# Graph layer on one core: row sums stored by SyncE instead of added by GpSimd, and a fifth of the lookup tables kept in SBUF

## The chip, the cores and the metric

One core of a Trainium2 chip runs the whole program. The metric is the device time of one execution in microseconds; the kernel before has a median of 24819.2 us over 10 runs (24803.0 to 24842.31). Engines are named as in the profile: PE is TensorE (matmul), PEld its weight loads, DVE VectorE, ACT ScalarE, POOL GpSimd, SP SyncE. SP computes nothing; it issues DMAs, as ACT and POOL can. "L391" is line 391 of the kernel before.

## The reference

A graph with 100000 nodes of 64 features has 3.3 million edges (1.6 million random pairs in both directions and one loop per node), sorted by the node they point to (`dst`). Each node's features are normalised and clipped at zero (`h`); the mean over a node's incoming edges goes through a linear layer, and is added to the input:

```python
h = jnp.maximum(_layernorm(x, axis=-1), 0.0)
local, nbr = h[dst], h[src]
y = jnp.einsum('ec,oc->eo', jnp.concatenate([local, nbr - local], axis=-1), W) + b
s = segment_sum(y, dst, 100000)
cnt = segment_sum(ones, dst, 100000)[:, None]
x = x + jnp.where(cnt > 0, s / jnp.maximum(cnt, 1.0), 0.0)
```

Since the layer is linear, what has to be summed over edges is only `h[src]` and a count: for each node the sum of some 33 rows picked at random from a table of 100000 rows.

## The kernel before, in words

**Stage 1, rows** (L269 to L310). `h` is computed and written to HBM as `h3`: each row is the float32 value split in three bf16 parts of 64, and ones for the count, 194 values (`CT`) of which 193 (`CE`) are used. A float32 array `acc` of 65 columns (64 sums and a count) is filled with zeros. At the end of the program `acc` is turned into means, multiplied by the weights and added to `x` (L983 to L1019).

The edges are summed in two ways at the same time.

**Chunks** (`chunks`, L345). The last 1.26 million edges are cut in 352 chunks of 3584 (28 columns of 128). For each column POOL issues an indirect DMA that gathers 128 rows of `h3` into `nb` (L391); DVE makes a one-hot matrix `hot` of the targets relative to the chunk's first node; PE multiplies the two into PSUM (`ps`, L396). A chunk covers at most 128 neighbouring nodes. Its base, the first node, is in `base_r` and `base_b`. When a chunk is done DVE reduces `ps` to `sums` (L407, L409), and later `addition` adds these 128 rows to `acc` by a POOL DMA with accumulation: an indirect one in the prologue (L366), one with a start row read from `base_r` in the loop (L371). The index arrays of a group of `KG` = 16 chunks are loaded at once (`load`, L348), two chunks ahead of their use. `nb` has 6 buffers of half a chunk (14 columns).

**Windows** (`quads`, L740). The first 2.04 million edges are cut in 256 windows of 7968 edges; a window covers at most 256 nodes (`CH`). Four windows make a set, of which there are 64. The edges of a window were sorted by their source in two lanes (`sort_lane`, mostly DVE and ACT) and spread out into index arrays in HBM (`fill_lane`; it also uses POOL gathers). For a set the kernel walks over all of `h3` in 157 steps of 640 rows, two steps at a time: the rows come as a table `tab` by SP (three steps in one load, 53 loads per set, L761); DVE makes one-hot matrices `gh` (L789) and `dh` (L340) from `srs` and `dt`, which SP loads too; PE picks the wanted rows (`gp`, L811, 12 matmuls for two steps), ACT copies them to `gs` (L813), and PE adds them to the four windows' sums (`total`, L819, 32 matmuls for two steps). At the end of a set DVE makes the four `wsums` (L839 to L845), and `addition` (L847) adds 256 rows of each to `acc` by a POOL DMA with accumulation (L849), from the start row in `wb_r`. `load` buffers are three deep, and SP's loads are issued 8 steps ahead (`AHEAD`).

**The order.** All engines run their instructions in the order in which the program emits them; only semaphores order the engines against one another. `chunks` is a generator that yields after each gather; the other stages call it to interleave gathers with their own work. In the prologue `gathers(ns)` (L873) emits one gather for each `GATHER` = 1250 ns of estimated work; a double step of the first four sets counts 2 x `STEP`. The prologue is: the two lanes' sort with chunks beside it (lane 1 also fills lane 0), then the sets 0 to 3 (`U0`) with the filling of lane 1, then `drain(ev)` emits what is left of the prologue's chunks (`PA`, 58 of them), and `add_now(True)` the additions. Then a loop runs three times (L909), each with 20 sets (`SB`) and 98 chunks (`KB`), the chunks' gathers spread evenly over the sets' steps, and at its end `drain` and `add_now(True)`; between two turns all engines meet.

Additions are put off: `add_later(due, ...)` queues one until 56 more gathers are emitted ((`LAG` - 1) x `J`), and `add_now` emits at most one in `GAP` = 8 gathers. `number` (L318) reads a start row into a register of the engine named. `odd` collects flags for inputs that don't fit the plan (a window with too many nodes and the like); if one is set, a loop at the end clears `acc` and does all edges again in a simple way (L937 and L947, zero turns here).

Of the kernel before, what the change touches and what calls it, by code (L numbers as in the profile page):

```python
# [27 lines left out]
P = 128  # L28
P = 128
# [5 lines left out]
KB = 98  # L35
U0 = 4
KG = 16
# [3 lines left out]
STEP = 1050  # L41
GAP = 8
# [52 lines left out]
def gnn_preln(ctx: ExitStack, tc, x, src_w, dst_w, src_p, dst_p, src_a, dst_a, wT, b, out, V, E):  # L95
# [50 lines left out]
    wb_d = dram.tile([SETS * W, 1], I32, name="wb_d")  # L146
# [28 lines left out]
    wb_r = consts.tile([1, SETS * W], I32, name="wb_r")  # L175
    turns = consts.tile([1, 2], I32, name="turns")
    ones = consts.tile([P, 1], F32, name="ones")
# [4 lines left out]
    odd = consts.tile([P, 1 + 5 * LANES], F32, name="odd")  # L182
# [129 lines left out]
    with tc.tile_pool(name="rows", bufs=6) as rows, \  # L312
# [5 lines left out]
        def number(at, engine, most):  # L318
            with tc.issue_after(last[engine].ins):
                return nc.values_load(at, engines=[engine], min_val=0, max_val=most)  # L320
# [5 lines left out]
        later = []  # L326
        count = [0, 0]
# [17 lines left out]
        def chunks(first, n, dynamic=None):  # L345


            def load(q):  # L348
# [11 lines left out]
                to = index.tile([P, KG], I32, name="to", bufs=3)  # L360
                nc.vector.tensor_scalar(to[:, :k], base_b[:, at], pcol, None, op0=ALU.add)
                return si, near, to

            def addition(q, rows_to, sums):
                if dynamic is None:
                    nc.gpsimd.indirect_dma_start(  # L366
                        out=acc, out_offset=bass.IndirectOffsetOnAxis(ap=rows_to, axis=0),
                        in_=sums, in_offset=None, compute_op=ALU.add)
                else:
                    at = number(base_r[0:1, ds(dynamic + q, 1)], POOL, V)  # L370
                    nc.gpsimd.dma_start(acc[ds(at, P)], sums, accum_op=ALU.add)  # L371
# [4 lines left out]
            for k in range(n * parts + 1):  # L376
                q, part = divmod(k, parts)
                u = q % KG
                if q < n:
                    if u == 0 and part == 0:  # L380
                        si, near, to = ahead
                    hot = rows.tile([P, JH, P], BF16, name="hot", bufs=4)
                    nb = rows.tile([P, JH, CT], BF16, name="nb")
                    with behind():
                        one_hot(hot, near[:, u, part * JH:part * JH + JH], P)
# [18 lines left out]
                if before is not None and before[2] == parts - 1:  # L404
                    sums = rows.tile([P, C1], F32, name="sums", bufs=LAG + 2)
# [4 lines left out]
                    add_later((LAG - 1) * J, lambda b=before[3], s=sums: addition(*b, s))  # L410
                if q < n:
                    before = (hot, nb, part, (q, to[:, u:u + 1]))
# [5 lines left out]
        def sort_lane(l, keys, piece, few, ps):  # L418
# [5 lines left out]
            nc.vector.tensor_scalar_min(wb[:, 0:1], wb[:, 0:1], float(V - CH))  # L424
# [315 lines left out]
        def quads(base, n):  # L740
# [4 lines left out]
            def fetch(t):  # L745
# [12 lines left out]
                if s < NCB and s % TG == 0:  # L758
# [4 lines left out]
                if s == NE // 2:  # L763
                    owns[u] = load.tile([P, W, NT, CT], BF16, name="own", bufs=1)
                    for i in range(W):
                        at = number(wb_r[0:1, ds((base + u) * W + i, 1)], SP, V - CH)
# [56 lines left out]
            def put(t):  # L823
# [12 lines left out]
                for i in range(W):  # L836
# [10 lines left out]
                    def addition(w=(base + u) * W + i, sums=sums):  # L847
                        at = number(wb_r[0:1, ds(w, 1)], POOL, V - CH)
                        nc.gpsimd.dma_start(acc[ds(at, CH)].rearrange("(b p) c -> p b c", p=P), sums, accum_op=ALU.add)  # L849

                    add_later((LAG - 1) * J, addition)
# [17 lines left out]
        with tc.tile_pool(name="few", bufs=1) as few:  # L869
# [14 lines left out]
            with tc.tile_pool(name="keys", bufs=2) as big, tc.tile_pool(name="piece", bufs=2) as piece, \  # L884
                    tc.tile_pool(name="fill", bufs=2) as fill, tc.tile_pool(name="sort_ps", bufs=2, space=PSUM) as ps:
                for l in range(NL):
                    rest = fill_lane(l - 1, fill, took) if l else iter(())
                    for i, ns in enumerate(sort_lane(l, big.tile([P, WL], F32, name="keys"), piece, few, ps)):
# [5 lines left out]
                        gathers(ns)  # L894
# [3 lines left out]
            with tc.tile_pool(name="load", bufs=3) as load, tc.tile_pool(name="hots", bufs=3) as hots, \  # L898
# [9 lines left out]
                add_now(True)  # L908
                with tc.For_i(0, (SETS - U0) // SB, 1) as g:  # L909
                    ev = chunks(None, KB, PA + g * KB)  # L910
                    next(ev)
                    owed = 0.0
                    for _ in quads(U0 + g * SB, SB):
# [5 lines left out]
                    add_now(True)  # L919

    with tc.tile_pool(name="few", bufs=1) as few, tc.tile_pool(name="w_ps", bufs=1, space=PSUM) as wps:
        worst = few.tile([P, 1], F32, name="worst")
# [136 lines left out]
```

## Time and profile before

The profile shows one execution. It took 24811.12 us, and the span of its instructions, from the first to the last, is 24809.4 us; the median of the 10 runs is 24819.2 us. Cut by what runs:

| stretch, us from the start | us | what runs | PE matmuls | POOL busy, us | granted PE clock | DMA, GB/s |
|---|---|---|---|---|---|---|
| 0 to 437 | 437 | rows | 1569 | 205 | 0.75 | 290 |
| 437 to 2720 | 2283 | sort, lanes 0 and 1, beside it 1267 gathers | 1190 | 1517 | 0.52 | 63 |
| 2720 to 4084 | 1364 | sets 0 to 3, beside it 284 gathers | 14408 | 526 | 0.74 | 176 |
| 4084 to 4201 | 117 | drain, 73 gathers | 162 | 83 | 0.54 | 35 |
| 4201 to 10968 | 6767 | loop, turn 1 | 73424 | 2868 | 0.75 | 171 |
| 10974 to 17729 | 6755 | loop, turn 2 | 73424 | 2866 | 0.75 | 172 |
| 17729 to 24482 | 6753 | loop, turn 3 | 73424 | 2865 | 0.75 | 172 |
| 24482 to 24809 | 327 | last stage | 1177 | 201 | 0.79 | 316 |

A row of the table comes from the view by stretches: busy time of each engine, the number of its instructions, the clock that the throttle granted to PE (1.00 is full speed), and what the DMA engines moved. "Busy" for POOL means here that it issues a DMA; such an issue takes 0.94 us for a gather, with 0.30 us to the next. The transfer itself runs on the DMA engines after that.

The DMAs that matter: `tab`, 3328 loads of 727.5 KB and 64 smaller ones, by SP; `srs`, 1216 of 512 KB, by SP; `nb`, 9856 gathers by POOL; the additions by POOL, 58 indirect ones in the prologue (1626 ns of POOL each in the median), 294 for chunks in the loop (1027 ns), 256 for windows (1372 ns). Of the idle time of an engine the profile names what ended it; "issue" stands where nothing that it records did.

### The profile page before, as it was taken

To read this page: it belongs to the slowest core of one execution; us is meant where nothing else is said; L and a number is where in the kernel's file an instruction comes from. 1 tells how busy PE (TensorE), PEld (TensorE's weight loads), DVE (VectorE), ACT (ScalarE), POOL (GpSimd) and SP (SyncE) were. 2 spreads that over 40 slices of the span, in tenths; PEclk is the share of its full clock that TensorE was granted. 3 is DMA by queue.
4 is the path that set the end of the run, shared out by engine and by line. 5 is a ranking of instruction groups with operands and counts; after the bars stand their busy time and mean duration, and the time that the engine had idled before them with its cause. 6 is when DMAs were issued, how large, how long until landed. Compare 5 with 4: busy or idle time off the path is not lost. (4 is left out here: it accounts for less than half of the span.)

```text
span 24809.4 us, 559362 instructions
## 1 busy us (share of the span) xinstructions
PE 15138.1 (61%) x238778; PEld 10860.3 (44%) x238778; DVE 11311.7 (46%) x15452; ACT 6041.3 (24%) x11710; POOL 11130.7 (45%) x11210
## 2 busy tenths in 40 slices
PE   4000365666666666656666666666566666666666
PEld 3000243444444444444444444444444444444445
DVE  6879543444444444434444444444344444444444
ACT  4333321222222222222222222222222222222222
POOL 5666534444444444434444444444344444444444
PEclk6555676777777777777777777777777777777777
DMA  6722454555555555555555555555555555555557
GB/s 232 101 44 46 106 176 146 175 174 172 173 174 171 173 172 172 171 161 174 172 173 172 174 175 173 172 170 174 160 176 171 174 174 172 174 173 172 171 172 250
DMA packets 1746424, 4097.89 MB, mean 165 GB/s; under 512 B 943899, under 2 KB 952230, under 8 KB 1738950
## 3 DMA queue, kind: packets, MB, share of 16 engines
q1 hardware_dynamic: 1182534, 3461.26, 42.0%
q0 software_dynamic: 454208, 535.92, 12.1%
q10 hardware_dynamic: 107168, 64.74, 1.4%
q8 instruction: 1877, 30.75, 0.5%
q14 instruction: 637, 5.22, 0.1%
HBM read 3880.72 MB, written 219.04 MB: 165 GB/s over the span
## 5 line engine op out<-in xcount | busy, mean ns | idle before, releaser
L391 POOL DMA_INDIRECT nb<-h,si x9856 | 9427.7, 957 | 11963.0 <-PE ps L396 8248.7
L811 PE MATMUL gp<-tab,gh 128*128 128x193 bf16 x60288 | 7547.4, 273 | 2523.7 <-issue 2270.7
L819 PE MATMUL total<-gs,dh 32*128 32x193 bf16 x160768 | 6516.7, 266 | 4168.3 <-issue 4146.2
L340 DVE TENSOR_TENSOR dh<-dt,c 128x1024 bf16<-128x1024 int16 x5056 | 3449.8, 682 | 12259.1 <-remote 7230.8
L813 ACT CAST gs<-gp 128x386 bf16<-128x386 f32 x10048 | 4767.2, 483 | 16503.6 <-remote 8963.7
L811 PEld LDWEIGHTS <-gh 128*128 128x128 bf16 x60288 | 5467.3, 106 | 4316.2 <-issue 3891.2
L819 PEld LDWEIGHTS <-dh 32*128 32x128 bf16 x160768 | 3912.0, 99 | 6384.1 <-issue 6320.6
L789 DVE TENSOR_TENSOR gh<-srs,c 128x1536 bf16<-128x1536 int16 x5056 | 4758.6, 941 | 23.3 <-PE gp L811 16.9
L396 PE MATMUL ps<-nb,hot 128*128 128x193 bf16 x9856 | 1923.3, 280 | 2526.4 <-DVE sums L409 1301.6
L396 PEld LDWEIGHTS <-hot 128*128 128x128 bf16 x9856 | 1045.6, 110 | 2715.5 <-DVE sums L409 1331.3
L455 ACT COPY tmp<-keys 128x1536 f32<-128x1536 f32 (+14 forms) x540 | 650.0, 1213 | 1286.3 <-issue 613.3
L456 DVE TENSOR_TENSOR keys<-tmp,keys 128x1536 f32<-128x1536 f32 (+14 forms) x540 | 756.1, 1419 | 91.6 <-issue 41.5
L457 DVE TENSOR_TENSOR keys<-tmp,keys 128x1536 f32<-128x1536 f32 (+14 forms) x540 | 755.6, 1418 | 16.0 <-remote 5.6
L340 DVE TENSOR_TENSOR hot<-near,c 128x1792 bf16<-128x1792 int16 x704 | 759.4, 1079 | 2.6 <-PE ps L396 2.0
L849 POOL DMA_DIRECT2D acc<-wsums x256 | 347.4, 1357 | 335.7 <-DVE wsums L845 216.2
L636 POOL DMA_INDIRECT kf<-ksort,at_i x322 | 309.6, 961 | 202.0 <-ACT k L677 96.9
L371 POOL DMA_DIRECT2D acc<-sums x294 | 301.1, 1024 | 212.1 <-DVE sums L409 203.1
L778 POOL DMA_INDIRECT rows_x<-h,xs x128 | 123.3, 964 | 358.5 <-DMA xs<-xs_d 292.6
L839 DVE SCALAR_TENSOR_TENSOR whole<-own,whole 128x193 f32<-128x193 bf16 x512 | 190.5, 413 | 162.4 <-ACT whole L835 161.2
L407 DVE TENSOR_REDUCE sums<-ps 128x64 f32<-128x192 f32 x352 | 123.0, 349 | 224.1 <-remote 165.6
L303 PE MATMUL o_ps<-w_own,hT 128*128 128x128 f32 x784 | 186.6, 376 | 14.6 <-ACT hT L298 14.1
L303 PEld LDWEIGHTS o_ps<-w_own,hT 128*128 128x128 f32 x784 | 155.1, 252 | 80.7 <-ACT hT L298 70.8
(174 smaller groups left out, 3522.3 us busy)
## 6 DMA issues: line engine op xcount, KB each, us to landing
tab<-tables SPq DMA_DIRECT2D x3328, 727.5 KB
srs<-sr_d SPq DMA_DIRECT2D x1216, 512.0 KB
nb<-h,si POOLq DMA_INDIRECT x9856
tables<-h ACTq DMA_DIRECT2D x157, 242.5 KB
h<-parts SPq DMA_DIRECT2D x28, 1358.0 KB
acc<-zeros SPq DMA_DIRECT2D x28, 910.0 KB
at<-acc SPq DMA_DIRECT2D x28, 910.0 KB
xt<-in_x SPq DMA_DIRECT2D x28, 896.0 KB
```

The costliest lines, as they stand in the source:

```text
L303: nc.tensor.matmul(o2[:, i], lhsT=hT[:, i], rhs=w_own.rearrange("p a c -> p (a c)"), start=False, stop=True)
L340: nc.vector.tensor_tensor(out.rearrange("p k (a d) -> p k a d", d=D), numbers[:, :, None].to_broadcast(shape), upto[:shape[0], :n].rearran ...
L391: last[POOL] = nc.gpsimd.indirect_dma_start(out=nb[:, j], out_offset=None, in_=h3, in_offset=bass.IndirectOffsetOnAxis(ap=si[:, u, at:at + ...
L396: nc.tensor.matmul(ps, lhsT=before[0][:, j], rhs=before[1][:, j, :CE], start=before[2] == 0 and j == 0, stop=before[2] == parts - 1 and j ...
L455: last[ACT] = nc.scalar.copy(tmp, lo)
L456: nc.vector.tensor_tensor(lo, tmp, hi, ALU.min)
L457: last[DVE] = nc.vector.tensor_tensor(hi, tmp, hi, ALU.max)
L789: nc.vector.tensor_tensor(gh[:, :m].rearrange("p c i b s -> p (c i) b s"), srs[u, s // SL][:, c:c + m].rearrange("p c i s -> p (c i) s")[: ...
L811: nc.tensor.matmul(gp[:, i], lhsT=ghots[t][:, i, b], rhs=row[:, b + i * (NB - NR), :CE], start=b == 0, stop=b == NR - 1)
L813: nc.scalar.copy(gs[t], gp)
L819: nc.tensor.matmul(total[:, i, to(b)], lhsT=hot[at, b * P:b * P + P], rhs=of[at], start=flags.get("start", False) and b == 0, stop=flags.g ...
L849: nc.gpsimd.dma_start(acc[ds(at, CH)].rearrange("(b p) c -> p b c", p=P), sums, accum_op=ALU.add)
```

## The change

The additions of POOL are replaced by plain stores of SP. Neighbouring chunks, and neighbouring windows, cover rows that overlap: the last node of one may be the first of the next, and a store overwrites. So each store (`put`) is followed by a copy of one row, the one at which the next chunk or window begins, to an array at the side (`shared`, to `side_c` or `side_w`) before the next store overwrites it. Both are emitted through `add_later`, 56 gathers after the sums and `GAP` = 4 later. All wait in order on `acc`: a copy for its put to land, the next put for the copy. At the end `add_side` adds the rows at the side to `acc`, with five indirect POOL DMAs with accumulation. The first three chunks (`EARLY`), whose rows the last windows may touch, keep their sums in SBUF, and POOL adds them after the loop. New flags in `odd` check that bases rise.

Four chunks of each loop turn move to the prologue (`KB` 98 to 94; `PA` becomes 70). To emit them there, `STEP` rises from 1050 to 1300, and each yield of lane 1 counts 350 ns more (`EXTRA`). `KG` falls from 16 to 8, and each 5th group of tables (`KEEP`), 11 of 53, is loaded once to `kept` ahead of the loop, and not again in the loop's sets.

```diff
-KB = 98
+KB = 94
-KG = 16
+KG = 8
-STEP = 1050
-GAP = 8
+STEP = 1300
+GAP = 4
+EARLY = 3
+EXTRA = 350
+KEEP = 5
...
+    side_w = dram.tile([SETS * W, C1], F32, name="side_w")
+    side_c = dram.tile([NMT * P, C1], F32, name="side_c")
...
-            def addition(q, rows_to, sums):
-                if dynamic is None:
-                    nc.gpsimd.indirect_dma_start(
-                        out=acc, out_offset=bass.IndirectOffsetOnAxis(ap=rows_to, axis=0),
-                        in_=sums, in_offset=None, compute_op=ALU.add)
-                else:
-                    at = number(base_r[0:1, ds(dynamic + q, 1)], POOL, V)
-                    nc.gpsimd.dma_start(acc[ds(at, P)], sums, accum_op=ALU.add)
+            def keep(q, sums):
+                c = ds(first + q if dynamic is None else dynamic + q, 1)
+                after = ds(first + q + 1 if dynamic is None else dynamic + q + 1, 1)
+
+                def put():
+                    at = number(base_r[0:1, c], SP, V)
+                    last[SP] = nc.sync.dma_start(acc[ds(at, P)], sums)
+
+                def shared():
+                    at = number(base_r[0:1, after], SP, V)
+                    last[SP] = nc.sync.dma_start(side_c[c], acc[ds(at, 1)])
+
+                add_later((LAG - 1) * J, put)
+                add_later((LAG - 1) * J + GAP, shared)
...
-                    add_later((LAG - 1) * J, lambda b=before[3], s=sums: addition(*b, s))
+                    if own:
+                        early.append(sums)
+                    else:
+                        keep(before[3], sums)
...
-        def quads(base, n):
+        def quads(base, n, kept=None):
...
-                if s < NCB and s % TG == 0:
+                if s < NCB and s % TG == 0 and kept is not None and s // TG % KEEP == 0:
+                    tabs[u, s // TG] = kept[:, s // TG // KEEP]
+                elif s < NCB and s % TG == 0:
...
-                    def addition(w=(base + u) * W + i, sums=sums):
-                        at = number(wb_r[0:1, ds(w, 1)], POOL, V - CH)
-                        nc.gpsimd.dma_start(acc[ds(at, CH)].rearrange("(b p) c -> p b c", p=P), sums, accum_op=ALU.add)
-
-                    add_later((LAG - 1) * J, addition)
+                    keep(u, i, sums)
+
+            def keep(u, i, sums):
+                w = ds((base + u) * W + i, 1)
+                after = ds((base + u) * W + i + 1, 1)
+
+                def put():
+                    at = number(wb_r[0:1, w], SP, V)
+                    last[SP] = nc.sync.dma_start(acc[ds(at, CH)].rearrange("(b p) c -> p b c", p=P), sums)
+
+                def shared():
+                    at = number(wb_r[0:1, after], SP, V + P)
+                    last[SP] = nc.sync.dma_start(side_w[w], acc[ds(at, 1)])
+
+                add_later((LAG - 1) * J, put)
+                add_later((LAG - 1) * J + GAP, shared)
...
-                        gathers(ns)
+                        gathers(ns + (EXTRA if l else 0))
...
+                tail = ExitStack()
+                stay = tail.enter_context(tc.tile_pool(name="stay", bufs=1))
+                kept = stay.tile([P, -(-NTB // KEEP), TG, NB, CT], BF16, name="kept")
+                for k in range(0, NTB, KEEP):
+                    m = min(TG, NCB - k * TG)
+                    nc.sync.dma_start(kept[:, k // KEEP, :m].rearrange("p c b f -> p (c b f)"),
+                                      tables[k][:, :m].rearrange("p c x -> p (c x)"))
                 with tc.For_i(0, (SETS - U0) // SB, 1) as g:
...
-                    for _ in quads(U0 + g * SB, SB):
+                    for _ in quads(U0 + g * SB, SB, kept):
...
+                for q, sums in enumerate(early):
+                    at = number(base_r[0:1, q:q + 1], POOL, V)
+                    nc.gpsimd.dma_start(acc[ds(at, P)], sums, accum_op=ALU.add)
...
+        def add_side(k, rows_of, to, a, z):
+            of = few.tile([P, C1], F32, name="side", bufs=NMT + SETS * W // P)
+            at = few.tile([P, 1], I32, name="side_at", bufs=NMT + SETS * W // P)
...
+            nc.scalar.dma_start(of[a:z], rows_of[k * P + a:k * P + z])
+            nc.scalar.dma_start(at[a:z], to[k * P + a + 1:k * P + z + 1])
+            nc.gpsimd.indirect_dma_start(out=acc, out_offset=bass.IndirectOffsetOnAxis(ap=at, axis=0),
+                                         in_=of, in_offset=None, compute_op=ALU.add)
+
+        for k in range(SETS * W // P):
+            add_side(k, side_w, wb_d, 0, P)
+        for k in range(NMT):
+            add_side(k, side_c, base_i.rearrange("m p -> (m p)")[:, None], 0 if k else EARLY, min(P, NCH - 1 - k * P))
```

## The prediction

> **What bounds it now.** I read the engine totals first: TensorE 61%, VectorE 46%, GpSimd 45%; no engine is full.
>
> ```profile
> PE 15138.1 (61%) x238778; PEld 10860.3 (44%) x238778; DVE 11311.7 (46%) x15452; ACT 6041.3 (24%) x11710; POOL 11130.7 (45%) x11210
> ```
>
> So I cut the span into stretches: us, then busy time and number of instructions of PE, PEld, DVE, ACT, POOL, then granted clock, DMA share, GB/s.
>
> ```profile
> 10974.00:17729.00 6755.00, 4521.19 (x73424) 3213.84 (x73424) 2779.48 (x3913) 1520.19 (x3220) 2866.20 (x2962) 0.75 0.57 172
> 10866.00:10924.00 58.00, 55.93 (x1235) 46.43 (x1233) 45.21 (x60) 26.04 (x54) 1.00 (x1) 1.00 0.86 287
> 8020.00:8032.00 12.00, 5.94 (x39) 2.80 (x38) 0.50 (x1) 0.96 (x2) 9.56 (x10) 0.53 0.48 108
> 7926.00:7934.00 8.00, 2.09 (x7) 0.64 (x7) 0.00 (x0) 0.00 (x0) 5.67 (x6) 0.50 0.38 122
> 3300.00:3800.00 500.00, 374.63 (x6724) 274.95 (x6722) 248.14 (x338) 142.34 (x299) 166.51 (x168) 0.81 0.66 208
> 437.00:2720.00 2283.00, 194.11 (x1190) 164.98 (x1190) 1894.63 (x2094) 825.09 (x914) 1516.97 (x1539) 0.52 0.39 63
> ```
>
> The first row is one loop iteration. The second is its end, where GpSimd is silent: 1235 matmuls in 58 us, 21.3 per us. In the third and fourth GpSimd issues gathers without a break, and PE makes 3.3 and 0.9 matmuls per us. The clock only halves (0.50 to 0.53 against 1.00); the rate falls to a sixth and below. PE's timeline inside such a burst shows single matmuls that waited for nothing that the profile names:
>
> ```profile
> 8018.91 0.32 PE L819 MATMUL total<-gs,dh 32*128 32x193 bf16 x4 [1.15 <-issue]
> 8020.34 0.29 PE L819 MATMUL total<-gs,dh 32*128 32x193 bf16 x3 [1.11 <-issue]
> 8021.06 0.32 PE L819 MATMUL total<-gs,dh 32*128 32x193 bf16 x1 [0.44 <-issue]
> ```
>
> The waits close the circle:
>
> ```profile
> POOL nb L391 <- PE ps L396: 8248.7, 546, 44.8
> PE gp L811 <- DMA tab<-tables: 100.4, 62, 36.4
> DVE rel L356 <- DMA di<-in_dst_p: 106.4, 20, 8.3
> SPq L761 <- PE gp L811: 7996.6, 2227, 153.5
> ```
>
> GpSimd waits 8.2 ms for PE to free gather buffers, then bursts, and PE nearly stands. So the times of the two *add up*. An iteration's 73424 matmuls at 21.3 per us are 3448 us. Its GpSimd work: 2744 gathers and 40 of `rows_x` at a pitch of 1.25 us, 3480, plus the adds, costed next at 236: 3716 us. 6755 less 3448 leaves 3307, so one us of GpSimd issue costs 3307/3716 = 0.89 us. The stretch 3300 to 3800 says the same: 6724 matmuls are 316 us, GpSimd's 166.5 busy plus about 161 pauses of 0.30 are 215, the rest of the 500 is 184: 0.86. At the margin, taking a us out of a burst costs PE only that burst's few matmuls: 1 - 3.3/21.3 = 0.85, or 1 - 0.9/21.3 = 0.96. I take **0.90**.
>
> **Adds leave GpSimd (loop).** This is the timeline around one add:
>
> ```profile
> 10840.92 0.94 POOL L391 DMA_INDIRECT nb<-h,si  x1 [0.31 <-issue]
> 10841.86 1.03 POOL L371 DMA_DIRECT2D acc<-sums  x1
> 10843.19 1.05 POOL L391 DMA_INDIRECT nb<-h,si  x1 [0.30 <-issue]
> 10844.55 0.99 POOL L391 DMA_INDIRECT nb<-h,si  x1 [0.30 <-issue]
> ```
>
> An add puts its own duration into the row of gathers, and about 0.15 into the next two. An iteration has 98 of `sums` (100.5 us) and 80 of `wsums` (108.7), with 178 x 0.15 = 27: 236 us. Times 0.90: -212.
>
> **Four chunks per iteration move to the prologue.** 112 gathers x 1.25 x 0.90 = 126, and 112 matmuls / 21.3 = 5: -131. Three iterations: 3 x 343 = **-1030** (at 0.85: -975; at 0.96: -1099).
>
> **Prologue.** It gets 12 chunks, 336 gathers, and loses 58 adds of 1.63 us.
> - Sort: `EXTRA` adds 350 ns to lane 1's 353 yields (270 merges, 8 pieces, 74 counts, 1): 124 us, 99 gathers of 1250 ns. 42 adds go, 68 us. Net +56 of GpSimd time in a stretch where GpSimd is taken for 1517 + 0.30 x 1497 = 1966 of 2283 us and VectorE for 83%. Half shows: +28. At most +56; at best -60, as adds that waited for sums (116 us in the whole prologue) no longer hold GpSimd.
> - The first four sets: `STEP` gives 316 double steps 2 x 250 ns more: 126 gathers. 126 x 1.25 x 0.90 + 126/21.3 = 148, less 10 adds x 1.63 x 0.90: +133 (125 to 145).
> - The other 111 gathers run in the drain, hidden by nothing: 139, less 5 adds: +131 (125 to 170, at the 1.60 us per gather that 4084 to 4201 shows).
>
> Together **+292** (190 to 371).
>
> **Stores on SyncE** cost nothing by themselves in my sum. The cover is SyncE's wait for PE to free table buffers, 8.0 ms above, and the distance in program order: 56 gathers to the put, 4 or more from put to copy. Behind a store that waits on SyncE stand the table, `srs` and `dt` loads; PE waits for those. Without that cover see the second rival. At an iteration's end nothing covers them:
>
> ```profile
> 17701.90 1.22 POOL L849 DMA_DIRECT2D acc<-wsums  x1 [17.55 <-DVE wsums L845]
> 17705.65 1.20 POOL L849 DMA_DIRECT2D acc<-wsums  x1 [2.53 <-DVE sums L409]
> 17709.36 1.18 POOL L849 DMA_DIRECT2D acc<-wsums  x1 [2.52 <-DMA acc<-wsums]
> ```
>
> One link, issue and landing, takes 3.7 us; five links follow the last set now, ten will (put and copy). No row shows SyncE storing to `acc`; I use 3.7: 5 x 3.7 x 3 iterations = **+55** (0 to 166, at twice 3.7).
>
> **KG 8** makes 12 index loads of an iteration instead of 7. Each holds VectorE, and PE behind it, for 106.4/20 = 5.3 us: 5 x 5.4 x 3 = **+81** (0 where a wait falls into a burst, to 166 with the prologue's five more at the longest wait, 8.3).
>
> **Kept tables.** Filling: 11 x 727.5 KB = 8.0 MB at 287 GB/s, **+28** (0 to 47, at 172 GB/s), since in SyncE's order it stands behind the prologue's last store and ahead of the loop's first index load. Gain: PE's waits for tables are 100 us in all, and 11 of 53 loads go: **-40** (0 to -100).
>
> **Tail.** Three early adds x 3.7, five side adds x (1.63 + 2.5 landing), loads before them 4.5: **+36** (25 to 60). The new checks are small VectorE work beside it.
>
> **Sum:** -1030 + 292 + 55 + 81 + 28 - 40 + 36 = -578 on the profiled span of 24809.4: 24231. That execution took 24811.1; the median of the runs is 24819.2, 9.8 over its span: **24240**. All bounds one way: -1099 + 190 - 100 + 25 = -984, 23835; the other: -975 + 371 + 166 + 166 + 47 + 60 = -165, 24654.
>
> **Rules that speak against it.** The rows have PE crawl beside GpSimd's DMA issue (3.3 against 21.3 matmuls per us). The Trainium skill, page "SBUF — State Buffer", section "Who interferes with whom", says that a DMA never contends with a compute engine and that only VectorE and GpSimd share a port. By it PE would not slow, the adds would be free and the result the first rival's. The trace disagrees; I follow it. "Trainium Kernel Development and Optimization", section "Key Constraints", says that issuing DMAs from another engine saves only the sequencer's issue time; here that very issue time is what I price at 0.90.
>
> **Rivals.**
> 1. *Adds were free*: the crawl belongs to the gathers' traffic alone. For: nearly all of a burst is gathers. Against: the add stands between two gathers and delays the next. Loop -3 x 131 = -393; prologue 62 + 148 + 139 = +349; the rest +160: +116, about **24935**. 6%.
> 2. *SyncE becomes the bound*: a copy of a shared row waits for its put to land, and the put stands behind queued tables. For: PE does wait for late tables, once 36.4 us. The loop has 3 x 178 x 2 = 1068 such stores; it decides from 578/1068 = 0.54 us of PE per store. If PE sees half a landing of 2.5 us: +1335, about **25580**. Against: SyncE's 8.0 ms of slack. 11%.
> 3. *Table traffic feeds the crawl*, and a fifth less eases it. For: DMA moves 108 to 122 GB/s in the slow rows. Against: from 8058 to 8066 it moved 52 and PE still made 2 matmuls per us. If a tenth of the 3307 us goes in each iteration: -990 more, about **23250**. 8%.
> 4. *It doesn't do what it says*: a base repeats, the new checks trip, and the fallback redoes everything: 1612 turns x 16 x (1.25 + 1.63) us = 74 ms. A window of 7968 edges at 33 per node spans some 241 nodes, so neighbours are far apart. 1%.
>
> **Numbers.** Forecast 74%; it is faster over its whole own range, 23835 to 24654. With 26% outside that, I let the range reach up over the first rival: 23830 to 24950 leaves out rivals 2 to 4, 20%. About 0.2% (50 us) is what a measurement tells from no change. Faster: forecast 74, the third 8. The first rival lies so near that a third of it falls within 0.2%: 2, with 1 for the forecast's upper edge; slower: the rest. Rounded: 0.81, 0.03, 0.16.
>
> **What would show it.** Right: iterations of about 6755 - 343 + 18 + 27 - 13 = 6444 us; the loop begins near 4520; GpSimd has gathers alone in the loop; PE still makes 1 to 3 matmuls per us in bursts and 21 outside. Wrong: PE waiting for `tab` behind stores on SyncE (rival 2); iterations near 6620 with bursts as long as now (rival 1); a higher PE rate inside bursts (rival 3).

## The result and the profile after

The changed kernel takes 25566.5 us (median of 8 runs, 25545.1 to 25589.4), the kernel before 24819.8 (28 runs): a ratio of 1.0299, 95% interval 1.0290 to 1.0308. It is slower by 3%, where 24240 was forecast. The profiled execution has a span of 25548.6 us, 739 more than before.

One thing has to be known to read what follows. The experiments were drawn onto ten different chips. On three of them the kernel before took 24527, 24787 and 24816 us, much as above; on seven it took 15364 to 15400. The program and its data were the same. In the first kind PE nearly stands while POOL issues gathers, as the prediction's rows show; I call that the crawl. In the second kind it doesn't. No chip was drawn twice, so that it is the chip which decides, and not the hour, isn't shown.

The view by stretches of the changed kernel, with the second turn and its end, where POOL is silent:

```profile
11491.00:18350.00 6859.00, 4367.30 (x73312) 3133.44 (x73312) 2777.41 (x3900) 1532.44 (x3220) 2523.21 (x2672) 0.74 0.49 145
11400.00:11466.00 66.00, 63.39 (x1411) 52.91 (x1410) 50.11 (x68) 29.31 (x61) 0.00 (x0) 1.00 0.66 207
```

POOL's busy time in a turn fell by 343 us, from 2866 to 2523 (that the prediction's gain of a turn is 343 us too is chance: it priced some 376 us of POOL's time at 0.90 and added 5), and PE still makes 21.4 matmuls per us where POOL is silent. Yet the turn grew by 104 us. The three turns take 6841, 6859 and 6844 us (6767, 6755 and 6753 before, with 6 more between the first two): +263 in all. The loop begins at 4650 instead of 4201: +449. The last stage has the other 27.

The waits say that nothing new is waited for on the path. Columns: who waited for whom, us in all, times, the longest:

```profile
POOL nb L403 <- PE ps L408: 8718.8, 509, 50.4
PE gp L828 <- DMA tab<-tables: 93.9, 74, 8.2
SPq L778 <- PE gp L828: 6488.9, 1556, 35.7
SPq L376 <- DVE sums L422: 584.8, 24, 117.6
SPq L380 <- DMA acc<-sums: 146.3, 86, 12.3
```

SP stands at the stores (L376) and the copies (L380), but it still waits 6.5 ms for PE, and PE waits no longer for tables than before (93.9 against 100.4 us). So what did PE lose? I split the second turn of both traces at POOL's runs of gathers, each taken from its first issue to 2 us after the end of its last (a run ends where POOL issues nothing for 3 us), and counted matmuls by their start:

```
                              before            after
in the runs                  4083 us           3653 us
  matmuls                   23658             13553
  per us                     5.79              3.71
outside                      2672 us           3206 us
  per us                    18.62             18.64
turn                         6755 us           6859 us
```

The runs became 430 us shorter, as meant. But inside them PE made 10105 matmuls fewer, and these cost 10105 / 18.63 = 542 us outside. 542 - 430, less 6 us for the 112 matmuls that moved to the prologue, is the +104 within 2 us.

Why fewer? In the trace of before, most runs of 14 gathers have one of two shapes: no add, or an add behind the second gather. One of each, by stretches, from the first issue to 2 us after the end of the last:

```profile
15217.43:15236.61 19.18, 7.59 (x83) 3.70 (x73) 2.59 (x4) 1.10 (x3) 13.22 (x14) 0.64 0.39 116
23391.77:23412.12 20.35, 10.47 (x143) 6.48 (x139) 3.95 (x7) 2.05 (x5) 14.40 (x15) 0.73 0.53 143
```

Count by the second pair, the weight loads, one for each matmul (the first counts also matmuls that are still running at the edge). With the add, POOL did one thing more, the stretch is 1.2 us longer, and PE made 139 matmuls instead of 73. This is no chance pair. Means of all such runs in the loops of the two traces: "us" goes from the first issue to the end of the last, "matmuls" counts 2 us further, and the other columns are matmuls per us in steps of 2 us from the first issue ("add third" stands behind the second gather):

```
                     runs  us     matmuls   0-2   2-4   4-6   6-8  8-10 10-12
before, no add        204  17.18   73.2    19.9   5.3   3.4   1.9   1.3   1.0
before, add third     159  18.35  137.6    15.4  19.1  17.1   5.7   2.5   2.1
before, add fourth     42  18.35  130.1    17.9   5.6  14.2  12.8   4.2   2.4
after, no add         451  17.18   72.1    17.9   6.4   3.3   1.9   1.3   1.3
```

The first two gathers of a run cost PE little; from the third on it crawls. An add there starts the count anew: two more cheap gathers. It costs 1.17 us and hands PE 64.4 matmuls, 3.0 us at 21.3 per us. After the change no run has one. That reading was mine from two traces, and the experiments had to test it.

### The profile page after: what moved, and what is told of

Same layout as the page of the kernel before. It is cut to its first block, busy times and chain, and to the rows that moved or that the text cites. A ratio compares the mean times of both kernels' runs of the same rounds, so it can differ in the third digit from the quotient of the medians.

```text
span 25548.6 us, 562905 instructions
## 1 busy us (share of the span) xinstructions
PE 14717.0 (58%) x238778; PEld 10633.3 (42%) x238778; DVE 11336.5 (44%) x15478; ACT 6077.5 (24%) x11710; POOL 10310.8 (40%) x10609
## 5 line engine op out<-in xcount | busy, mean ns | idle before, releaser
L836 PE MATMUL total<-gs,dh 32*128 32x193 bf16 x160768 | 6234.0, 263 | 4403.8 <-issue 4387.9
L828 PE MATMUL gp<-tab,gh 128*128 128x193 bf16 x48408 | 6043.6, 269 | 2723.3 <-issue 2485.8
L828 PEld LDWEIGHTS <-gh 128*128 128x128 bf16 x60288 | 5339.8, 104 | 5224.1 <-issue 4829.1
L836 PEld LDWEIGHTS <-dh 32*128 32x128 bf16 x160768 | 3832.0, 99 | 6298.3 <-issue 6252.2
L828 PE MATMUL gp<-kept,gh 128*128 128x193 bf16 x11880 | 1531.0, 271 | 546.5 <-issue 533.6
L736 POOL DMA_INDIRECT kx<-ksort,xat x128 | 120.8, 944 | 89.5 <-DVE xat L733 44.4
```

Of the source, the lines that this page charges most:

```text
L828: nc.tensor.matmul(gp[:, i], lhsT=ghots[t][:, i, b], rhs=row[:, b + i * (NB - NR), :CE], start=b == 0, stop=b == NR - 1)
L836: nc.tensor.matmul(total[:, i, to(b)], lhsT=hot[at, b * P:b * P + P], rhs=of[at], start=flags.get("start", False) and b == 0, stop=flags.g ...
```

## The experiments

All times of a run are beside the kernel before on the same chip.

**Pauses and stores put back (a chip without the crawl).** Each edit is to the changed kernel, the fourth to the one before:

```diff
 # e1, behind each put (e2: the memset there; e3, e4: the memset after every 2nd gather)
+with tc.issue_after(last[POOL].ins):
+    nc.gpsimd.dma_start(aside_c[turn[0] % 4], sums)
...
+last[POOL] = nc.gpsimd.memset(pause, 0.0)
```

> The changed kernel, and beside each store that SyncE makes GpSimd now issues a plain store of the same sums (nothing is added) to memory that nobody reads: 178 short DMA issues per turn are back on GpSimd, at the places where the adds stood. Theory A (a break in a run of gathers is worth more than it costs: each of the old adds gave TensorE 69 matmuls, some 3.2 us, for 2.7 us of a longer burst): the turns go back from 6850 us to about 6760, the total from 25567 to about 25300. Rival B (the prediction's price: 1 us of GpSimd issue costs 0.90 us, and something else of the change ate the gain): 178 issues at 1.2 us by 0.90 add 190 us, the turns take about 7040 us and the total is about 26140.

> The changed kernel with a GpSimd memset of a tile that nobody reads (128 x 1024 floats, estimated at 1 us) at the same 178 places per turn; no DMA is added. Theory A, if any break in the run of gathers does it: turns of about 6770 us, total about 25300. Theory A', if it must be a DMA of another kind: the memset costs its own time, turns of about 7010 us and a total of about 26050, while the run with the plain store goes down. Rival B: 178 times 1 us by 0.90 is +160 us, turns of about 7010 us, total about 26050, and the run with the plain store goes up as well.

> The changed kernel with the same memset after every second gather of the loop: 1316 of them per turn. Theory A: no gather is later than the second of its run, where TensorE still issued 13 to 20 matmuls per us; 73312 matmuls at 13 to 15 per us are 4900 to 5600 us per turn, and the total is about 20900 us (19700 to 21800). Rival B: 1316 us more of GpSimd by 0.90 add 1180 us to each turn: turns of 8040 us, total about 29100.

> The kernel before with the same memset after every second gather of its loop (1372 per turn). Theory A: the crawl goes here too, turns of 5000 to 5700 us and a total of about 20600 us. Rival B: 1372 us by 0.90 add 1235 us to each of the three turns: total about 28500.

Before took 15378 us here, so no total fits either theory. The ratios: 1.0094 (1.0077 to 1.0110), 1.0052 (1.0035 to 1.0069), 1.1474 (1.1452 to 1.1497) and 1.2199 (1.2175 to 1.2224). Without the crawl pauses buy nothing. To see what differs, both kernels were run unedited.

> The changed kernel once more, unedited. The first four experiments ran on a chip on which the kernel before takes 15378 us, not 24819, and in their traces TensorE issues about 20 matmuls per us inside the runs of gathers, where the traces of the prediction show 1 to 3. Theory A (the loss of 3% belongs to the crawl: without it the change gains what leaves GpSimd): the plain stores of the first experiment (0.58 us and some issue each, 534 of them) and the memsets of the second (about 1 us each) are taken off again, and this kernel runs at 15100 to 15350 us where before takes 15378, a ratio of 0.982 to 0.998. Rival B (the change itself costs 3%, through SyncE's stores or the prologue): a ratio of 1.01 to 1.03 on either chip. Where before takes 24.8 ms again, both expect 25567 us.

> The kernel before, unedited, for its trace on the chip of this series. Theory A: gathers take 0.95 us here as well and GpSimd's busy time is 11130 us as it was; what differs is TensorE's rate inside the runs of gathers, 18 to 21 matmuls per us for 5.7, and with it 9400 us of span. Rival: the gathers themselves, or the transfers, are quicker on this chip.

> The kernel before without the 178 adds per turn that its loop issues on GpSimd: the sums are computed and go nowhere, so most of the output's edge sums are left out. Theory A where TensorE crawls in the runs of gathers (before at 24.8 ms): each add was worth 69 matmuls, 3.2 us, for 2.7 us, so the turns grow by 90 us and the total to about 25100. Theory A where it doesn't crawl (before at 15.4 ms): 343 us of GpSimd per turn come off the engine that is then the busiest, 0.9 us each, so the total falls by 500 to 930 us to 14450 to 14900. Rival B: the total falls by about 930 us on either chip.

The gathers of the kernel before, by groups (busy us, mean ns of one, idle time before it and what ended it), on the prediction's chip and on this one:

```profile
L391 POOL DMA_INDIRECT nb<-h,si x9856 | 9427.7, 957 | 11963.0 <-PE ps L396 8248.7 <-issue 2794.7 <-DMA si<-in_src_p 321.1
```

```profile
L391 POOL DMA_INDIRECT nb<-h,si x9856 | 9430.5, 957 | 3289.7 <-issue 2819.1 <-PE ps L396 234.6 <-DMA nb<-h,si 97.1
```

A gather takes POOL 957 ns on both. One turn of before, then of after, without the crawl:

```profile
7480.00:11280.00 3800.00, 3395.29 (x73424) 2781.42 (x73424) 2779.58 (x3913) 1540.85 (x3220) 2866.86 (x2963) 0.97 0.94 306
```

```profile
7650.00:11357.00 3707.00, 3358.18 (x73312) 2785.77 (x73312) 2766.03 (x3900) 1542.46 (x3220) 2527.29 (x2672) 0.97 0.84 267
```

The same 73424 matmuls and the same POOL work fit in 3800 us instead of 6755, since PE makes 19.4 matmuls per us inside the runs. The changed kernel took 15425.6 us, a ratio of 1.0022 (1.0011 to 1.0032): turns some 93 us shorter, and the loop begins 271 us later (3965 for 3694). Neither theory's ratio was met: the turns gain without the crawl, as A said, but the prologue takes it back. Taking the loop's adds away alone (e7, which leaves their sums out of the output) gave 0.9789 (0.9773 to 0.9806), -327 us. That is 109 us for the 230 us of POOL's busy time that leave a turn (128 by the two traces): half of the prediction's price even here, and less than A expected.

**The parts of the change one by one (without the crawl).** e8 undoes the split of the chunks, e9 also the kept tables and `KG`; e10 adds short pauses:

```diff
 # e8 and e9
-KB = 94
+KB = 98
-STEP = 1300
+STEP = 1050
-EXTRA = 350
+EXTRA = 0
 # e9 besides: KG = 16, no kept tables
 # e10: the changed kernel with
+if dynamic is not None and count[0] % 4 == 0:
+    breathe()
```

> The changed kernel with the old split of the edge chunks: 98 of them in each turn instead of 94, and the old shares of the gathers in the prologue (112 gathers per turn go back from the prologue into the loop). On the chips of this series (before at 15.4 ms) the loop of the changed kernel begins 271 us later than before and its turns are 99 us shorter. Theory A (the moved gathers cost the prologue all of the 271 us and are worth little in the loop, by the run without adds 0.6 us per us of GpSimd): the loop begins at about 3700 us, turns of 3780 us, total about 15390. Rival B (gathers are worth 0.9 in the loop): turns of 3820 us, total about 15500. If the prologue's 271 us come from elsewhere, the loop still begins at 3965 us and the total is 15650. Where TensorE crawls (before at 24.8 ms): about 25600 by either.

> The kernel before with the first part of the change alone: the sums are stored by SyncE and the shared rows added at the end, the old split of the chunks, index batches of 16, no tables kept in SBUF. The run without adds took 15066 us on a chip of this series, where before takes 15393. Theory A (SyncE's stores cost the loop nothing): that time and some 30 us for the adds of the shared rows at the end, about 15100 us, a ratio of 0.978 to 0.985; this would beat both kernels. Rival B (SyncE becomes the bound, since the stores queue among its loads): 15250 to 15500 us. Where TensorE crawls (before at 24.8 ms): theory A 25100 to 25300 us (an add was worth more than it cost), rival C (adds cost 0.9 of their time) about 24000 us.

> The changed kernel with a shorter GpSimd memset (128 x 256 floats, about 0.25 us) after every fourth gather of the loop, 658 per turn. Where TensorE crawls (before at 24.8 ms), theory A (any break in a run of gathers ends the crawl for two or three gathers): about 10 matmuls per us within the runs, turns of 5200 to 5700 us, total 20600 to 22100; rival B: 658 times 0.25 us by 0.9 are +150 us per turn, total 26000. Where it doesn't crawl (before at 15.4 ms): GpSimd has some 360 us per turn to spare (3700 less 2523 of work and 0.31 us of issue for each of 2632 gathers), the memsets fit into them, and the total is 15420 to 15700 by both.

e8 took 15345.1 us (0.9976, 0.9967 to 0.9986): the loop began at 3685 and turns took some 3764, below A's 3780. So the moved gathers cost the prologue all of the 271 us and saved some 66 a turn. e10 took 15425.5 (1.0033, 1.0021 to 1.0045), the changed kernel's own time: its 658 memsets a turn are hidden. e9 was a miss: 16075.8 (1.0448, 1.0431 to 1.0465), worse than B's range. PE's wait for tables in the run without adds, and in e9 with SP's own waits:

```profile
PE gp L810 <- DMA tab<-tables: 628.7, 690, 17.4
```

```profile
PE gp L828 <- DMA tab<-tables: 1369.2, 827, 17.8
SPq L376 <- DVE sums L422: 721.6, 33, 72.9
SPq L876 <- DMA acc<-wsums: 529.8, 159, 5.9
SPq L380 <- DMA acc<-sums: 339.8, 135, 12.6
```

Where the loop runs this fast, SP stands 870 us for stores to land before their copies, the tables behind come late, and PE's wait for them doubles. This is the prediction's second rival, on chips other than those it was priced for. With the kept tables and `KG` = 8 (e8) PE's wait is 772 us and the total 731 us lower; which of the two did it wasn't tested.

**Copies later, with and without short pauses.** The edit to e8, and e12 with the memset of e10 besides:

```diff
-add_later((LAG - 1) * J + GAP, shared)
+add_later((LAG - 1) * J + 16, shared)
```

> The changed kernel with the old split of the chunks (the run that took 15345 us where before takes 15382), and each copy of a shared row is due 16 gathers after its store instead of 4. In that run SyncE stood 805 us at the copies, waiting for the store before them to land, and the table loads behind them came late (PE waited 772 us for tables). Theory A (the stores cost the loop what SyncE stands in order at the copies; its own issue, 1.4 ms of a 3.8 ms turn, isn't the bound): the waits at the copies all but go, and the total falls to 15050 to 15250 us, a ratio of 0.979 to 0.991: faster than both kernels. Rival B (it is the traffic or the issue of the stores and copies): 15300 to 15400. Where TensorE crawls (before at 24.8 ms): 25400 to 25700 by both.

> The same, with the short GpSimd memset (128 x 256 floats) after every fourth gather of the loop. Where it doesn't crawl the memsets cost nothing that could be measured in the changed kernel (15426 us with and without them), and this run should be within 100 us of the one beside it. Where TensorE crawls (before at 24.8 ms): theory A (any break in a run of gathers ends the crawl for two or three gathers) 20600 to 22100 us, rival B (a memset costs its time) about 26000 us.

These fell on a chip that crawls (before 24527): 25346.1 (1.0332, 1.0315 to 1.0349) and 25194.6 (1.0272, 1.0255 to 1.0289). e11 is 54 us below its range there, which was set for a before of 24.8 ms; as a ratio to before (1.023 to 1.036) it is inside. A turn of it, with all 98 chunks of before and no adds on POOL:

```profile
11105.00:18035.00 6930.00, 4432.48 (x73424) 3159.92 (x73424) 2782.82 (x3918) 1527.07 (x3220) 2627.61 (x2784) 0.74 0.49 144
```

POOL does 239 us less than in a turn of before, and PE makes 3.80 matmuls per us inside the runs: 6930 us. e12 felled my theory as it stood, that any break ends the crawl. The pauses gained 0.6%, not 13% or more. The memsets (times, shortest, median and longest ns), then one run with four of them by stretches:

```profile
L340 POOL MEMSET pause<- x2058: 325/330/707, 4202.3 to 24722.3; 128x256 f32 x188
```

```profile
6538.30:6558.36 20.06, 9.07 (x96) 4.85 (x96) 2.56 (x6) 1.18 (x3) 14.53 (x18) 0.70 0.44 132
```

Four pauses of 0.33 us bring 92.0 matmuls in the mean of 231 such runs, for 76.1 in e11's 457 runs of 14 on the same chip: 0.75 us of PE for 0.88 of POOL, so they repay about their own time and no more. Where the 0.6% comes from, these runs don't say. So either the length of a break matters, or its kind, or its place, or the add had never been the cause. One kernel put all of these side by side.

**Eight treatments in one loop.** To the changed kernel, by the number `q` of the chunk:

```diff
+def between(kind, j):
+    with tc.issue_after(last[POOL].ins):
+        if kind == 1 and j == 1 or kind == 3 and j % 2 == 1:
+            last[POOL] = nc.gpsimd.memset(pause[:, :1024], 0.0)
+        if kind == 2 and j == 1 or kind == 7 and j == 6:
+            last[POOL] = nc.gpsimd.memset(pause, 0.0)
+        if kind == 4 and j == 1:
+            last[POOL] = nc.gpsimd.dma_start(aside[turn[0] % 4], few_c)
+        if kind == 5 and j == 1 or kind == 6 and j == 6:
+            last[POOL] = nc.gpsimd.dma_start(extra[turn[0] % 4], few_c, accum_op=ALU.add)
...
+between(q % 8, j)
```

> The changed kernel with eight treatments side by side in its loop, one for every eighth chunk (two runs of 14 gathers each): none; a GpSimd memset of 1 us behind the second gather; one of 2 us there; one of 1 us behind every second gather; a plain store of a constant tile there; an adding store of it to memory nobody reads there, which is the form of the old adds; the adding store behind the seventh gather; the memset of 2 us behind the seventh. Only its trace counts, and where TensorE crawls (before at 24.5 to 24.8 ms) above all. In the trace of before, a run of 14 gathers without an add took 17.2 us, and TensorE issued 73 matmuls from its start to 2 us after its end; with an add behind the second gather 18.3 us and 138 matmuls. Theory A (the add itself did that: it costs 1.1 us and hands TensorE 65 matmuls, 3.1 us): the runs with the adding store behind the second gather show 125 to 150 matmuls again, the untreated 70 to 75. If a DMA of another kind does it, the plain store too; if time without a gather does it, the memsets of 1 and 2 us too (95 to 150); if the place matters, the same behind the seventh gather give less than 100. Rival B (an add only stood where TensorE was quick anyway, for another reason): the adding store gives 73 plus what its own slot lasts, under 100 matmuls.

> The kernel of the mixed run once more, since that run fell on a chip without the crawl (before at 15364 us), where its question can't be put. Where TensorE crawls (before at 24.5 to 24.8 ms), theory A: 125 to 150 matmuls from the start of a run of 14 gathers to 2 us after its end where an adding store stands behind the second gather, 70 to 75 where nothing does; the plain store and the memsets show whether it is the kind of work or the time without a gather, the treatments behind the seventh gather whether the place matters (under 100). Rival B: under 100 matmuls with the adding store as well.

e13 met a chip without the crawl (15493.6, before 15364.2), where the question can't be put. e14 met one with it: 24199.8 us where before took 24787.3, one run each. Typical runs by stretches: a whole untreated chunk (28 gathers); then, in runs of 14, the adding store behind the second gather, the plain store there, memsets of 1 and 2 us there; then the adding store and the 2 us memset behind the seventh:

```profile
6765.91:6802.57 36.66, 8.84 (x80) 4.66 (x81) 6.67 (x10) 0.96 (x2) 26.43 (x28) 0.61 0.38 96
22043.80:22064.11 20.31, 10.80 (x149) 6.02 (x138) 3.53 (x5) 2.05 (x5) 14.35 (x15) 0.78 0.53 150
9746.98:9766.77 19.79, 8.92 (x104) 4.60 (x97) 4.55 (x8) 1.18 (x3) 13.82 (x15) 0.67 0.35 87
20160.59:20180.61 20.02, 10.61 (x134) 5.93 (x126) 4.23 (x6) 2.04 (x5) 14.20 (x15) 0.76 0.45 131
14365.20:14386.06 20.86, 10.52 (x155) 6.14 (x144) 5.61 (x8) 1.96 (x5) 15.04 (x15) 0.74 0.39 99
19401.08:19421.41 20.33, 9.80 (x110) 5.27 (x103) 2.38 (x5) 1.15 (x4) 14.37 (x15) 0.63 0.40 101
13610.38:13631.24 20.86, 11.16 (x153) 7.65 (x147) 4.43 (x7) 2.21 (x6) 15.04 (x15) 0.75 0.40 106
```

The means; "net" is matmuls over 73.2 at 21.3 per us, less the time beyond 17.18 us. The first row is from the kernel before, since e14 has no untreated run of exactly 14: its untreated chunks ran as 28 gathers, with 79 matmuls in the mean of 27, as many as such runs of the changed kernel on the prediction's chip (79):

```
treatment of a run of 14           runs   us    matmuls   net us
none (before)                       204  17.18    73.2      0
adding store behind 2nd              69  18.31   138.0    +1.9
plain store behind 2nd               38  17.79    96.1    +0.5
memset, 1 us, behind 2nd             63  18.01   125.2    +1.6
memset, 2 us, behind 2nd             60  18.86   144.0    +1.6
adding store behind 7th              66  18.33    99.1    +0.1
memset, 2 us, behind 7th             60  18.86   143.0    +1.6
```

The adding store gives the 138 matmuls of the old adds, with data and an address that have nothing to do with them: it was the add that did it. A memset, which moves no data, does nearly the same, so the kind isn't what counts. Length is: the run grows by 0.6 us with the plain store, 0.8 with the short memset, 1.1 with the add, 1.7 with the long memset, and the gain goes with it. So is place: deep in a run an add's 1.1 us no longer does, the long memset's 1.7 still does. Chunks with a memset behind every second gather ran at 13 to 20 matmuls per us throughout (means in steps of 2 us).

**Pauses everywhere.** The kernel of e3 once more, then e11 with the 1 us memset after every second gather, twice:

> The changed kernel with a 1 us GpSimd memset after every second gather of its loop, as in the third experiment, which fell on a chip without the crawl. In the mixed run, where TensorE crawled, chunks so treated ran at 12 to 21 matmuls per us throughout, and 28 gathers with their memsets gave TensorE about 19 us more than they cost. Theory A, on a chip that crawls (before at 24.5 to 24.8 ms): 94 chunks of 19 us off each turn of 6850, so turns of about 5060 us (4900 to 5500) and a total of 20100 us (19600 to 21500), faster than both kernels by 13 to 20%. Rival B, what is gained in the runs is lost outside them, or to another engine: above 22500. Where it doesn't crawl: 17650 us again.

> The changed kernel with the old split of the chunks and the copies 16 gathers after their stores (25346 us on a chip that crawls, where before took 24527), and a 1 us GpSimd memset after every second gather of the loop. Theory A, on a chip that crawls: the loop begins at 4190 us as in that run and a turn of 98 chunks takes about 5200 us instead of 6930, a total of about 20150 us (19500 to 21600). Rival B, the gain in the runs is lost outside them or to another engine: above 22500. Where it doesn't crawl, GpSimd bounds the loop: 4444 us a turn by 98/94 are 4630, a total of about 17930 us.

> The kernel of the run before (old split, later copies, a 1 us memset after every second gather), for a chip that crawls. Theory A there (before at 24.5 to 24.8 ms): turns of about 5200 us and a total of about 20150 us (19500 to 21600); rival B above 22500. Where it doesn't crawl: 17930 us again.

e15 and e17 met chips without the crawl: 17640.0 (1.1467, 1.1448 to 1.1486) and 17931.5 (1.1649, 1.1615 to 1.1683), as expected there. e18 met one with it: 19099.3 us where before took 24815.5, a ratio of 0.7695 (0.7672 to 0.7717). A turn of it, and its memsets by groups:

```profile
9030.00:13880.00 4850.00, 3951.25 (x73424) 2960.52 (x73424) 2811.45 (x3918) 1457.14 (x3220) 3962.95 (x4156) 0.96 0.68 206
```

```profile
L340 POOL MEMSET pause<- 128x1024 f32 x4116 | 3988.5, 969 | 1.7
```

POOL does 1335 us more per turn than in e11, and the turn falls from 6930 to 4850 us, 350 below what I expected; PE makes 15.0 matmuls per us while POOL works. On a chip that crawls it beats the kernel before by 23%, and the changed one, 3% behind that, by more; on one that doesn't it costs 16%. With the pauses the two kinds of chip lie 6.5% apart (19099 and 17932 us), not 60%.

**Copies later, where nothing crawls.** The kernel of e11:

> The changed kernel with the old split and the copies 16 gathers after their stores once more: the question it was made for can only be put on a chip that doesn't crawl, and the first time it fell on one that does. There the run with the copies 4 gathers behind took 15345 us, before 15382, the run without any adds or stores 15066, and the stores alone, with the tables loaded anew each time, 16076. Theory A (the stores cost the loop what SyncE stands in order at the copies, 805 us there): the waits all but go, total 15050 to 15250 us, faster than both kernels. Rival B (it is the traffic or the issue of the stores): 15300 to 15400. Where TensorE crawls: 25346 us again.

15187.2 us, a ratio of 0.9872 (0.9855 to 0.9888): there it beats both kernels. SP's waits with the copies 4 gathers behind (e8) and 16 (this run):

```profile
SPq L876 <- DMA acc<-wsums: 508.5, 161, 6.0
SPq L380 <- DMA acc<-sums: 296.9, 129, 12.1
```

```profile
SPq L876 <- DMA acc<-wsums: 367.4, 141, 6.4
SPq L380 <- DMA acc<-sums: 299.1, 96, 12.8
```

The total is A's, its mechanism only in part: the waits fell by 139 us, not nearly to nothing, and the time by 158. What the rest of the stores' cost is, traffic or issue, stays open.

## Why the prediction was wrong

**The step that failed** is the price at the margin: "taking a us out of a burst costs PE only that burst's few matmuls", 0.90 us per us of POOL's issue, whatever is taken out. For gathers deep in a run that is roughly right (-102 of -131 a turn, below). For an add it has the wrong sign: the prediction took PE's crawl in a run for a property of POOL's being busy, while it comes from gathers in a row, and an add among the first of them puts it off. The mean of 0.89 that the prediction found was true of a turn as a whole; it was used for the one part of that work which wasn't like the rest. The rows that would have told it were there: runs of gathers with an add and without, 138 against 73 matmuls.

**Adds off POOL**, -212 a turn: between e11's 98-chunk turn and that of before, the runs are 286 us shorter and hold 9213 matmuls fewer, 9213 / 18.7 = 492 us: +206 (+175 measured, between two chips whose times for before differ by 1.2%; `KG` and the kept tables are in it too). The 67 adds of a turn behind the second or third gather of a run of 14 account for 4210 of the 9213. **Moved gathers**, -131 a turn: the runs of the changed kernel are 144 us shorter than e11's and hold 892 matmuls fewer, 780 without those of the moved chunks' own: -102 of 131. Three turns of +206 and -102 are +312; +263 was measured, -1030 forecast.

**Prologue**, +292 (and +28 for the kept tables): the loop began 449 later, not 320. Sort +76 for +28, the first sets +221 for +133, the drain +151 for +131. Of its terms, 349 for the moved gathers and -57 for adds that leave, both were too good: e11, which has no adds on POOL here either but the old split, began its loop near 4185, so the split cost some 415 to 465 us (its chip is 1.2% quicker) and the adds' leaving saved 16 us at most. Without the crawl the split cost 271; which part of the gathers' price was too low isn't shown. The 16 adds of windows that left the prologue too (1.37 us each) were not in the sum.

**SyncE**, nothing in the loop: right where PE crawls, by the waits above. The +55 for the ends of the turns wasn't due: from the last `total` matmul of a turn to the first of the next took 52 and 50 us before, 45 and 46 after. The second rival's 25580 is close to the result by chance: PE did not wait for tables. Where nothing crawls its mechanism is real (e9).

**Small terms.** `KG 8`: VectorE's waits for `di` went from 106 to 204 us in 20 and 36 waits, 5.7 us each as sized. Kept tables: they were loaded at 3410 to 3463, beside other work, so +28 wasn't due, and PE's table waits fell by 7 us, not 40. Tail: +27 for +36.

**The rivals.** *Adds were free* came nearest in kind, and was given 6%; its turns of 6620 still lie 230 us below the measured ones, since the adds were worth more than nothing. *Table traffic feeds the crawl*: with a fifth of the table loads gone, runs without an add hold 72 matmuls, as before (73). The Trainium skill, page "SBUF — State Buffer", section "Who interferes with whom", says that TensorE and ScalarE never wait on anyone at SBUF's ports. The chips without the crawl, where PE keeps 19.4 to 19.9 matmuls per us beside the gathers (e1, e5, e6, e8, e13, e19), show nothing against it; on the others PE falls to 1 to 3, by whatever way.

Not shown: what in a chip makes it crawl, and why two gathers pass before it sets in. No run took the adds alone away on a chip that crawls (e7 and e9 met others): their worth there rests on e14's treated runs and on e11. That the adds of the windows, which stood at many places, did the same as those of the chunks is argued from the sums.

## What to carry to other kernels

A mean price per us of an engine's work holds for removing an average us of it. Before using it, split the stretch by what is to be removed: here runs with an add against runs without were both in the first trace, and one held nearly twice the matmuls of the other. When an engine slows another down, ask what ends the slowness; a pause, or work of another kind in the right place, may be worth more than the time it takes. And treatments side by side in one loop settle more than a run each, above all when the next run may meet another chip.

## What the runs showed of the hardware

- The same program takes 24.5 to 24.8 ms on some chips and 15.4 on others, with the same durations of gathers (957 ns) on both. Which kind a chip is can't be told from the program, and a change can lose on one and gain on the other: e18 0.77 and, as e17, 1.16.
- Where it shows, the crawl sets in with the third indirect gather in a row: 20 matmuls per us fall to 5, and to 1 some 8 us into the run. It outlasts the last gather by 2.5 to 3 us after a run of 14, by 4.5 us after one of 28.
- Breaks of 0.33 us repaid about their own cost and no more; a memset of 1 us behind the second gather was worth 2.4 us of PE; one that lengthened the run by 1.7 us was worth 3.3 behind the second and behind the seventh alike.
